# The attention denominators as four array tiles of 32 columns, with one reciprocal and a spread by DMA

## Chip, cores, metric

One core of one Trainium2 chip. The metric is the device time of one execution in microseconds, the median of several executions.

## The reference, cut to what matters

A batch of 32 graphs with 512 nodes and 512 features passes two layers. The change lies in the first, an attention with 8 heads of 64 features under an adjacency mask, in 32-bit floats throughout:

```python
scores = einsum('bqhd,bkhd->bhqk', q, k) / sqrt(64)
scores = scores + (1.0 - adj)[None, None, :, :] * -1e9
attn = softmax(scores, axis=-1)
out = einsum('bhqk,bkhd->bqhd', attn, v).reshape(b, n, d)
x = x + (out @ Wo + bo)
```

## The kernel before

The softmax has no maximum subtracted; it is exp of masked scores, and the division comes after the product with the values. Two heads, a *pair* of heads j of 4, are handled together: head s of the pair has partitions 64s to 64s+63. For each pair and batch (128 times) there are

- `scores`: keys on partitions, 512 queries along the row; the mask added by VectorE, exp by ScalarE, and the four exps of a pair summed by VectorE into `es`;
- `values`: the product with v into the bank `po`, copied by ScalarE to `o`;
- `finish`: the denominators. The sum of `es` over its 128 partitions is a product with a matrix of ones, which also copies the sum to 64 rows of each head, just where `o` has that head's features. PSUM (`psum.tile`) is the memory that takes TensorE's results, used here in banks of 512 columns.

```python
def finish(b, j, st):
    need("rd")
    pd = psum.tile([P, N], F32, name=f"pd_{b}_{j}", tag="pd")
    for s in range(2):
        nc.tensor.matmul(
            pd[s * HD : (s + 1) * HD, :], ones[:, :HD], st["es"][j][:, s, :], start=True, stop=True
        )
    pe(0.95)
    o = st["o"][j // 2][:, j % 2, :]
    rd = wtile([P, N], f"rd_{b}_{j}", "rd", 1)

    def divide(k):
        nc.vector.reciprocal(rd[:, ts(k, H)], pd[:, ts(k, H)])
        if k:
            then("rd", rest)

    def rest():
        junk = wtile([P, N], f"rj_{b}_{j}", "rj", 1, BF16)
        nc.scalar.activation(junk, rd, AF.Copy, accum_out=rsum[:, b, j : j + 1])
        nc.gpsimd.tensor_tensor(o, o, rd, op=ALU.mult)

    finished.add((b, j))
    release()
    for k in range(2):
        later("rd", 0.0, gap(b, (j + 1) % NP) + 3.0, 1.7, lambda k=k: divide(k))
```

Here P is 128, N is 512, H is 256 and HD is 64. The order of each engine's instructions is set by hand, with a small model of time while the program is built: `pe(us)` says that TensorE has so much more work, `later(key, wait, by, cost, fn)` lets a VectorE instruction go in where the model finds room, and `then(key, fn, wait)` puts out what follows VectorE's work. None of these numbers is a wait on the chip; they set order alone. What an engine waits for on the chip are semaphores, in the order of its own instructions.

The queries of the next batch are multiplied by an edge mask before scores can use them:

```python
nc.gpsimd.tensor_tensor(qh, qh, edge8[:, ts(k, H)], op=ALU.mult)       # proj_q
```

and in the output projection (`out_proj`) GpSimd adds one partial product to the residual, after which VectorE adds further ones from PSUM and so frees the bank that TensorE's last product of that projection needs:

```python
nc.gpsimd.tensor_tensor(r, r, q, op=ALU.add)                           # more(q_)
nc.vector.scalar_tensor_tensor(r, p_, 1.0 / VS, r, op0=ALU.mult, op1=ALU.add)   # add(i, k, p)
```

Another GpSimd instruction is the second layer's last addition, `y += x1`, ahead of the store of the output.

Of the kernel before, what the change touches and what calls it, by code (L numbers as in the profile page):

```python
# [9 lines left out]
F32 = mybir.dt.float32  # L10
BF16 = mybir.dt.bfloat16
I32 = mybir.dt.int32
AF = mybir.ActivationFunctionType
# [7 lines left out]
P = 128  # L21
HD = 64
# [13 lines left out]
H = 256  # L36
# [25 lines left out]
def kernel(  # L62
# [23 lines left out]
    nc = tc.nc  # L86
    B, N, D = x.shape
    T = N // P
    C = D // P
    NP = D // P  # L90
# [3 lines left out]
    def ctile(shape, name, dt=F32):  # L94
        return const.tile(shape, dt, name=name, tag=name)
# [8 lines left out]
    ones = ctile([P, P], "ones")  # L104
# [18 lines left out]
    rsum = ctile([P, B, NP], "rsum")  # L123
# [24 lines left out]
    psum = fast.enter_context(tc.tile_pool(name="psum", bufs=1, space=bass.MemoryType.PSUM))  # L148

    def wtile(shape, name, tag, bufs, dt=F32):  # L150
        return work.tile(shape, dt, name=name, tag=tag, bufs=bufs)
# [7 lines left out]
    def run_spare(i):  # L159
        _, ready, cost, fn, _ = spare.pop(i)  # L160
        clock["dve"] = max(clock["dve"], ready) + cost
        fn()

    def pe(us):

        clock["pe"] += us
        till = clock["pe"] + (1.0 if at_ends[0] else 0.4)
        while True:
            due = [i for i, (_, t, _) in enumerate(ends) if t <= till]
            fits = [  # L170
                (by, i) for i, (_, t, cost, _, by) in enumerate(spare)
                if max(clock["dve"], t) + cost <= till
            ]
            if due:
                ends.pop(due[0])[2]()
            elif fits:
                run_spare(min(fits)[1])
            else:
                return
# [5 lines left out]
    def later(key, wait, by, cost, fn):  # L185

        now = max(clock["dve"], clock["pe"])
        spare.append((key, now + wait, cost, fn, now + by))

    def then(key, fn, wait=0.0):  # L190

        ends.append((key, clock["dve"] + wait, fn))

    def need(key):

        waits = at_ends[0] and key not in ("e", "es") and any(e[0] == key for e in spare + ends)
        run_all(key)
        if waits:
            clock["pe"] = max(clock["pe"], clock["dve"])
# [326 lines left out]
    def release():  # L526
        while held:
            held.pop(0)()

    def gap(b, j):  # L530
        return GAPS.get(b, GAP)[j]
# [68 lines left out]
    def finish(b, j, st):  # L600

        need("rd")
        pd = psum.tile([P, N], F32, name=f"pd_{b}_{j}", tag="pd")
        for s in range(2):
            nc.tensor.matmul(  # L605
                pd[s * HD : (s + 1) * HD, :], ones[:, :HD], st["es"][j][:, s, :], start=True, stop=True
            )
        pe(0.95)
        o = st["o"][j // 2][:, j % 2, :]
        rd = wtile([P, N], f"rd_{b}_{j}", "rd", 1)  # L610

        def divide(k):
            nc.vector.reciprocal(rd[:, ts(k, H)], pd[:, ts(k, H)])  # L613
            if k:
                then("rd", rest)

        def rest():
            junk = wtile([P, N], f"rj_{b}_{j}", "rj", 1, BF16)
            nc.scalar.activation(junk, rd, AF.Copy, accum_out=rsum[:, b, j : j + 1])  # L619
            nc.gpsimd.tensor_tensor(o, o, rd, op=ALU.mult)  # L620

        finished.add((b, j))
        release()
        for k in range(2):
            later("rd", 0.0, gap(b, (j + 1) % NP) + 3.0, 1.7, lambda k=k: divide(k))

    def residual(b, st, i, tag="x1", bufs=3):

# [198 lines left out]
    def denominators(b, j):  # L827
        done = (b, j - 1) if j else (b - 1, NP - 1)
        if done[0] in states:
            finish(*done, states[done[0]])  # L830
# [336 lines left out]
```

## Time and profile before

| | before |
|---|---|
| median | 3678.0 us (3676.8 to 3679.0) |
| one batch in the steady part | 112.12 us, of which TensorE is busy 111.67 |
| denominators' product, start to next start | 0.910 us |
| GpSimd's multiply after the second reciprocal | 0.14 us in three places of a batch, 3.40 in one |

The steady part is about 28 of 32 batches; there a batch's period repeats to 0.01 us. The prediction below shows the lines and how they are read.

### The profile page before, as it was taken

How to read it: one execution, taken by the hardware profiler on the slowest of the kernel's cores; microseconds unless marked ns; L12 is line 12 of the kernel's file. 1: busy time of each engine (PE TensorE's matmuls, PEld its weight loads, DVE VectorE, ACT ScalarE, POOL GpSimd, SP SyncE). 2: the span in 40 equal slices, each digit the busy share in tenths (PEclk: the TensorE clock that was granted, in tenths of full speed). 3: DMA queues.
4: the chain of work that ended last, by engine and by line, in shares of the span. 5: the costliest groups of instructions: out<-in, count | busy, mean ns of one | idle time of the engine just before them, and what ended most of it. 6: DMA issues, size and time to landing. Idle time of an engine off the chain costs nothing. (4 is left out here: it accounts for less than half of the span.)

```text
span 3676.4 us, 58866 instructions
## 1 busy us (share of the span) xinstructions
PE 3606.2 (98%) x24310; PEld 1875.1 (51%) x24310; DVE 2802.5 (76%) x4119; ACT 1398.2 (38%) x2086; POOL 1147.1 (31%) x965
## 2 busy tenths in 40 slices
PE   9999999999999999999999999999999999999986
PEld 5545554555554555545555545555455555455532
DVE  6977777787777877777877778777778777787783
ACT  3433334334333433343333334333434343343331
POOL 5423333223333222332233332323332333323241
PEclk9999999999999999999999999999999999999998
DMA  3001111101111011111011110011110111100100
GB/s 130 18 7 35 38 38 35 33 9 38 38 38 35 10 32 38 38 35 38 4 38 38 38 35 14 28 38 38 35 38 4 38 38 38 35 18 24 32 27 27
DMA packets 71074, 120.58 MB, mean 33 GB/s; under 512 B 11856, under 2 KB 15952, under 8 KB 70800
## 3 DMA queue, kind: packets, MB, share of 16 engines
q1 hardware_dynamic: 69216, 114.91, 9.9%
q8 instruction: 193, 3.16, 0.4%
q10 hardware_dynamic: 1376, 1.57, 0.1%
q14 instruction: 81, 0.66, 0.1%
q0 software_dynamic: 208, 0.27, 0.0%
HBM read 83.11 MB, written 33.62 MB: 32 GB/s over the span
## 5 line engine op out<-in xcount | busy, mean ns | idle before, releaser
L620 POOL TENSOR_TENSOR oT<-oT,rd 128x512 f32<-128x512 f32 x128 | 167.2, 1306 | 1527.1 <-DVE rd L613 1524.5
L567 ACT ACTIVATE e<-e 128x1024 f32<-128x1024 f32 x512 | 541.0, 1057 | 196.0 <-DVE e L552 160.0
L552 DVE TENSOR_TENSOR e<-ps,nmT 128x1024 f32<-128x1024 f32 x384 | 455.1, 1213 | 101.9 <-PE ps L542 101.8
L542 PE MATMUL ps<-qT,kT 64*128 64x512 f32 x2048 | 483.4, 606 | 12.7 <-DVE e L552 12.7
L590 PE MATMUL po<-e,v 128*64 128x512 f32 x2048 | 463.1, 593 | 0.0
L51 PE MATMUL pg<-at,hn 128*64 128x512 f32 x2048 | 449.7, 598 | 13.2 <-DVE dmax L775 13.2
L51 PE MATMUL py<-w,gT 128*64 128x512 f32 x2048 | 447.4, 595 | 0.1
L613 DVE RECIPROCAL rd<-pd 128x256 f32<-128x256 f32 x256 | 435.0, 1729 | 0.0
L804 POOL TENSOR_TENSOR y<-y,x 128x512 f32<-128x512 f32 x128 | 193.2, 1509 | 544.9 <-DVE y L802 489.9
L542 PEld LDWEIGHTS ps<-qT,kT 64*128 64x128 f32 x2048 | 184.2, 186 | 309.4 <-issue 214.9
L564 DVE TENSOR_TENSOR es<-es,e 128x1024 f32<-128x1024 f32 x254 | 316.6, 1246 | 13.2 <-ACT e L567 0.6
L51 PEld LDWEIGHTS pg<-at,hn 128*64 128x64 f32 x2048 | 148.9, 138 | 307.5 <-issue 307.5
L51 PEld LDWEIGHTS py<-w,gT 128*64 128x64 f32 x2048 | 148.1, 138 | 293.9 <-issue 292.3
L590 PEld LDWEIGHTS po<-e,v 128*64 128x64 f32 x2048 | 157.8, 138 | 235.1 <-issue 225.4
L598 ACT COPY oT<-po 128x512 f32<-128x512 f32 x128 | 73.8, 576 | 388.2 <-PE po L590 388.2
L714 DVE CUSTOM_DVE_ANT_0 scr<-hn,wa_r 128x512 f32<-128x512 f32 x256 | 169.9, 719 | 49.0 <-ACT hn L701 49.0
L619 ACT ACTIVATE rj<-rd 128x512 bf16<-128x512 f32 x128 | 80.7, 630 | 327.5 <-DVE rd L613 327.4
L741 ACT ACTIVATE at<-at 128x512 f32<-128x512 f32 x128 | 80.4, 628 | 286.3 <-DVE at L737 286.3
L800 ACT ACTIVATE y<-py,rd 128x512 f32<-128x512 f32 x128 | 87.6, 685 | 261.2 <-PE py L51 253.0
L564 DVE TENSOR_TENSOR es<-e,e 128x1024 f32<-128x1024 f32 x127 | 180.9, 1424 | 0.7 <-PE pd L605 0.7
L639 POOL TENSOR_TENSOR x<-x,c_row 128x512 f32<-128x512 f32 x128 | 176.9, 1403 | 0.0
L321 POOL TENSOR_TENSOR rs<-rs,mhalf 128x2 f32<-128x2 f32 (+1 forms) x97 | 78.7, 811 | 306.9 <-DVE rs L320 305.8
(189 smaller groups left out, 5726.5 us busy)
## 6 DMA issues: line engine op xcount, KB each, us to landing
x<-in_x_dram SPq DMA_DIRECT2D x128, 256.0 KB, 3.0
out_dram<-y SPq DMA_DIRECT2D x128, 256.0 KB, 2.1
x<-in_x_dram SPq DMA_DIRECT2D x63, 512.0 KB, 4.2
s<-row_s SPq DMA_DIRECT2D x32, 256.0 KB, 4.2
adj<-in_adj_dram SPq DMA_DIRECT2D x4, 256.0 KB, 7.1
w<-in_L_gnn_W_dram SPq DMA_DIRECT2D x1, 1024.0 KB, 7.9
wk<-in_L_gnn_Wk_dram ACTq DMA_DIRECT2D x3, 256.0 KB, 8.9
wq<-in_L_gnn_Wq_dram SPq DMA_DIRECT2D x3, 256.0 KB, 7.6
```

The lines of the kernel that those rows point to most:

```text
L51: nc.tensor.matmul(out[s : s + HD], lhsT[:, s : s + HD], rhs, start=start, stop=stop, skip_group_check=onto)
L542: nc.tensor.matmul(ps[s], st["kT"][j][rows, ts(k, P)], st["qT"][j][rows, :], start=True, stop=True)
L552: nc.vector.tensor_tensor(e, p, nmT[:, k, :].unsqueeze(1).to_broadcast([P, 2, N]), op=ALU.add)
L564: (nc.gpsimd if early else nc.vector).tensor_tensor(es, one, e, op=ALU.add)
L567: nc.scalar.activation(e, e, AF.Exp)
L590: nc.tensor.matmul(po[s * HD : (s + 1) * HD, :], v[k // 2][:, k % 2, (2 * j + s) * HD : (2 * j + s + 1) * HD], e[k][:, s, :], start=k == 0 ...
L613: nc.vector.reciprocal(rd[:, ts(k, H)], pd[:, ts(k, H)])
L620: nc.gpsimd.tensor_tensor(o, o, rd, op=ALU.mult)
L639: nc.gpsimd.tensor_tensor(r[:, t, :], r[:, t, :], c_row, op=ALU.add)
L714: nc.vector.tensor_tensor_reduce(scr, st["hn"][t], r, 1.0, 0.0, op0=ALU.mult, op1=ALU.add, accum_out=st["s12"][:, g, t : t + 1],)
L800: nc.scalar.activation(y, p, AF.Exp, scale=r)
L804: nc.gpsimd.tensor_tensor(y, y, x1_of(st, t), op=ALU.add)
```

## The change

Its intent: with 32 columns of ones in place of 64, four tiles of the array can work at once, each on one head and one half of the queries. TensorE then streams 256 columns in place of 512. The result is [128, 256], so one reciprocal does for two. But each quarter of 32 rows now holds one head's and one half's denominators and has to be brought to two groups of 32 rows each of `rd`: eight DMAs.

```diff
-        pd = psum.tile([P, N], F32, name=f"pd_{b}_{j}", tag="pd")
+        pd = psum.tile([P, N], F32, name=f"pd_{b}_{j}", tag="pd")[:, :H]
         for s in range(2):
-            nc.tensor.matmul(
-                pd[s * HD : (s + 1) * HD, :], ones[:, :HD], st["es"][j][:, s, :], start=True, stop=True
-            )
-        pe(0.95)
+            for k in range(2):
+                r = (2 * s + k) * 32
+                nc.tensor.matmul(
+                    pd[r : r + 32, :], ones[:, :32], st["es"][j][:, s, ts(k, H)], start=True, stop=True
+                )
+        pe(0.5)
         o = st["o"][j // 2][:, j % 2, :]
-        rd = wtile([P, N], f"rd_{b}_{j}", "rd", 1)
-        def divide(k):
-            nc.vector.reciprocal(rd[:, ts(k, H)], pd[:, ts(k, H)])
-            if k:
-                then("rd", rest)
+        rq = wtile([P, H], f"rq_{b}_{j}", "rq", 1)
+        def divide():
+            nc.vector.reciprocal(rq, pd)
+            then("rd", rest)
         def rest():
-            junk = wtile([P, N], f"rj_{b}_{j}", "rj", 1, BF16)
-            nc.scalar.activation(junk, rd, AF.Copy, accum_out=rsum[:, b, j : j + 1])
+            nc.scalar.activation(pd, rq, AF.Copy, accum_out=rsum[:, b, j : j + 1])
+            rd = wtile([P, N], f"rd_{b}_{j}", "rd", 1)
+            for s in range(2):
+                for k in range(2):
+                    r = (2 * s + k) * 32
+                    for h in (s * HD, s * HD + 32):
+                        nc.sync.dma_start(rd[h : h + 32, ts(k, H)], rq[r : r + 32, :])
             nc.gpsimd.tensor_tensor(o, o, rd, op=ALU.mult)
-        for k in range(2):
-            later("rd", 0.0, gap(b, (j + 1) % NP) + 3.0, 1.7, lambda k=k: divide(k))
+        later("rd", 0.0, gap(b, (j + 1) % NP) + 3.0, 1.7, divide)
```

## The prediction

> **What bounds the kernel now.** I read the page's busy shares first, then the two last full periods before the middle of the run (one batch each, cut at the start of the same denominators' product in successive batches), then the list of TensorE's own waits, then the timeline around one denominators' product.
>
> ```profile
> PE 3606.2 (98%) x24310; PEld 1875.1 (51%) x24310; DVE 2802.5 (76%) x4119; ACT 1398.2 (38%) x2086; POOL 1147.1 (31%) x965
> ```
> ```profile
> 1309.70:1421.82 112.13, 111.68 (x754) 58.16 (x753) 86.51 (x128) 43.56 (x66) 34.23 (x29) 1.00 0.10 31
> 1421.82:1533.94 112.12, 111.67 (x754) 58.20 (x753) 86.52 (x128) 43.56 (x66) 34.22 (x29) 1.00 0.10 31
> ```
> ```profile
> PE pg L51 <- DVE dmax L775: 13.2, 2, 11.1
> PE ps L542 <- DVE e L552: 12.7, 32, 1.5
> PE pe L51 <- DVE as L748: 10.6, 1, 10.6
> PE pd L605 <- DVE rd L613: 10.4, 2, 5.5
> ```
>
> In the windows the first figure after the stretch is its length, the next TensorE's busy time, then weight loads, VectorE, ScalarE and GpSimd. A batch takes 112.12 us and TensorE works 111.67 of them; VectorE 86.52, so it has some 25 us free per batch. The period repeats to 0.01 us, so no variable wait lies in it. TensorE's waits for other engines sum to under 60 us in the whole run, and the two on the reciprocal (line 613, 10.4 us) are single events in batch 1 and in the tail. So the steady stage is bound by TensorE's stream; only what shortens the stream shortens the time, and 32 x 112.12 = 3588 of 3678 us are that stage.
>
> The product that is changed, with what stands before and after it:
>
> ```profile
> 1530.31 3.71 PE L542 MATMUL ps<-qT,kT 64*128 64x512 f32 x16
> 1533.94 1.08 PE L605 MATMUL pd<-es,ones 128*64 128x512 f32 x4
> 1534.86 1.90 PE L51 MATMUL x_k<-hT,wk 128*64 128x256 f32 x16
> ```
> ```profile
> 1533.94 0.20 PEld L605 LDWEIGHTS pd<-es,ones 128*64 128x64 f32 x4 [0.76 <-issue]
> ```
>
> Modelled ends overlap, so I count from start to start: 1534.86 - 1533.94 = 0.91 us is what the product takes from the stream (median of all 128: 0.910). It is 2 matmuls, but 4 records: each 32-bit matmul runs as two passes. The single records start at 0, 7, 481 and 488 ns: both column tiles' first passes together, then both second passes. A following slot of the same shape takes 429 ns for 512 columns and 215 ns for 256. The first slot is 52 ns longer, and the two weight loads of one tile start 54 ns apart, so this is the first load of 64 columns, which nothing hides. The last score slot before it is 519 ns and not 429: about 92 ns when the layout of the array changes (64 rows by 128 columns to 128 by 64). Wherever the layout changes in this trace I find that same 92 to 94 ns (scores to product, product to scores, to and from the transposes), followed by a longer first slot; where the products have one shape there is neither.
>
> **What the Trainium skill says.** (1) "TensorEngine Tiling (Array Packing)", Key Properties: a change of tiling mode drains the engine, and different tiles load weights and multiply in parallel. The trace agrees: the 92 ns above, and two tiles that start 7 ns apart. That page lists 128x32 with four tiles. (2) "TensorE: Matmul & The Clock Gate", LDWEIGHTS: a load takes its columns over 1.2 per ns, 53 ns for 64; the trace has 54. For 32 columns that is 27 ns, an estimate. (3) The same page, Measured speedup vs the span model: three column tiles of 32 gained 2.38x. No part of the kernel before uses four tiles, so this case doesn't yet show that four run abreast. (4) "DMA: Bandwidth & Descriptors", Anatomy of one DMA: a fixed cost of about 2 us for each. The trace has 2.1 us from issue to landing for 256 KB out, 1.4 for 2 KB.
>
> **The change part by part.**
>
> TensorE. Four tiles of 32 columns with 256 queries each in place of two of 64 with 512. If all four run abreast: first slot 215 + 27 = 242 ns, second 215, four starts 7 ns apart 14 ns more than two; 471 ns. But products before and after are in 128x64, and now the array changes twice: the drain ahead of it is already paid after scores, a new one of 93 ns follows, and the next product's first slot becomes 52 ns longer. 471 + 93 + 52 = 616 ns in place of 910: 0.294 us saved for each, 128 x 0.294 = 37.6 us. In four cases the product follows a 128x64 product and the front change is new too: 4 x 0.145 = 0.6. Net 37.0 us, all on the path that sets the end.
>
> VectorE.
>
> ```profile
> L613 DVE RECIPROCAL rd<-pd 128x256 f32<-128x256 f32 x256 | 435.0, 1729 | 0.0
> L620 POOL TENSOR_TENSOR oT<-oT,rd 128x512 f32<-128x512 f32 x128 | 167.2, 1306 | 1527.1 <-DVE rd L613 1524.5
> L619 ACT ACTIVATE rj<-rd 128x512 bf16<-128x512 f32 x128 | 80.7, 630 | 327.5 <-DVE rd L613 327.4
> ```
>
> One reciprocal of 128x256 in place of two: 128 x 1.73 = 221 us less VectorE, 6.9 us a batch. It lies beside TensorE, which waits for VectorE 0.4 us a batch at most, so it is worth nearly nothing in the steady stage. In batch 1 and the tail, where the product waited 5.5 and 4.9 us for the earlier reciprocal, some 1.7 us each can come back. ScalarE's check runs over 256 elements in place of 512: by its 630 ns some 0.2 us less each, off the path.
>
> DMA. Eight issues a product from SyncE, 1024 in all, 32 KB each, 32 MB together on a queue that has 10% of the engines' time.
>
> ```profile
> 1512.81 0.33 SPq L805 DMA_DIRECT2D out_dram<-y  x1
> 1516.79 0.86 SPq L328 DMA_DIRECT2D x<-in_x_dram  x2
> ```
> ```profile
> out_dram<-y SPq DMA_DIRECT2D x128, 256.0 KB, 2.1
> row_s<-s SPq DMA_DIRECT2D x32, 2.0 KB, 1.4
> ```
>
> Issues back to back come some 0.4 us apart: 8 x 0.4 = 3.2 us, and about 1.8 us for the last to land. GpSimd's multiply can start 5.0 us after the reciprocal in place of 0.14; the one reciprocal less takes 1.7 back, so 3.3 us later. What follows on GpSimd waits with it. Per batch the four places are: the combinations for the output projection, finished 35 us before their use; the residual's bias, not urgent; the combinations for the keys, of which the first is wanted about 10 us after it is ready; and the queries' multiply by the edge mask, ready at 1447.7 where the scores start at about 1450.8, 3 us of slack with some gap between the two multiplies to absorb part of the delay. So the delay mostly hides; I put 5 us in all (0.15 us a batch) for places where it doesn't. In the tail the combinations after the last product do set TensorE's start (a wait of 3.7 us at line 51), so about 3 us are lost there against some 5 us that the reciprocals free in head and tail: net 2 us gained.
>
> Sum: 3678.0 - 37.0 - 2.0 + 5.0 = 3644.0 us.
>
> **The rivals.**
>
> First, the four tiles don't run abreast. The passes stand in the program tile by tile, and a queue that looks past only one blocked pass would give pairs: three slots (242 + 215 + 215 = 672, + 145 = 817 ns), 0.09 us saved, 12 us: about 3669 with the rest. Two full pairs one after the other: 242 + 3 x 215 + 145 = 1032 ns, 16 us slower: about 3697. For it: nothing here shows four tiles. Against it: after each change of layout four weight loads start within 61 ns and the second tile's first pass overtakes the first tile's second. A milder form: the diagonal's products of 64 columns take 119 ns a slot of two records, some 60 ns each, not their streaming time. If that is a floor for each record, a slot of four is 238 ns: 0.25 saved, 3650.
>
> Second, the transfer becomes the bound. SyncE's queue is in order, and the rd pieces can stand behind a store that waits for GpSimd, or the row of logits (line 134), for which the queue waited 745 us in 32 times. Then GpSimd stands still, with it the queries or the variance's power, and VectorE behind that, and the scores. 1 us a batch would be 32 us, about 3676; beyond that it turns slower. For it: small slack at the queries. Against it: the multiply already waited 1524.5 us for the reciprocal in 110 cases without reaching TensorE, and VectorE has 7 us more room a batch.
>
> Third, VectorE's relief shows. If the 221 us had been holding TensorE, time could fall by over 100 us. The 0.45 us per batch in which TensorE is not busy speaks against it.
>
> **Range and chances.** Four abreast, delays hidden: 3630 to 3650, some 65%. The record floor or a partial overlap: 3650 to 3672, 15%. Four not abreast, or the transfer in the way: 3670 and up, 17%. Better than 3628 needs more than the stream can give. So 3628 to 3684 for 8 in 10. Over 2% faster is under 3604.5: 0.57 us from each product of 0.91, more than its four-tile form leaves; 0.03. Over 2% slower is above 3751.6: 2.3 us lost in each batch, only with the transfer in the way; 0.05.
>
> **What would show it.** Right: starts of the eight matmul records within some 25 ns in two groups 240 ns apart, 0.62 us from the product's start to the next one's, a 52 ns longer first slot in what follows; a period of about 110.9 us at a TensorE share still above 99%; VectorE near 80 us a batch; eight transfers 0.4 us apart and the multiply some 5 us after the reciprocal, with no new wait on TensorE's list. Wrong: three or four groups of starts; a wait of the scores on queries or mask sums that comes from GpSimd; a period that varies from batch to batch.

## The result, and the profile after

3853.8 us (3840.0 to 3860.2, four runs) against 3678.0: ratio 1.0473, 95% interval 1.0443 to 1.0503, slower by 4.7%. (Ratios are the mean time of one kernel's runs over that of the other's of the same rounds, so not quite the ratio of the medians.) The result is correct.

First the product itself, in the timeline of TensorE and of its weight loads of the changed kernel (start us, length us, engine, line, operation, operands):

```profile
1141.61 0.64 PE L608 MATMUL pd<-es,ones 128*32 128x256 f32 x8
1142.18 1.95 PE L51 MATMUL x_k<-hT,wk 128*64 128x256 f32 x16
```
```profile
1141.61 0.16 PEld L608 LDWEIGHTS pd<-es,ones 128*32 128x32 f32 x8 [0.76 <-issue]
```

From start to next start 0.57 us (median of all 128: 0.569), where 0.91 was. The eight records start at 0, 7, 13, 20 and 240, 247, 253, 260 ns: four tiles abreast. The first slot after it is 52 ns longer. This is what was predicted, to 5 ns. Yet the whole is slower. The busy shares, and two periods of one batch:

```profile
PE 3615.3 (94%) x24822; PEld 1783.0 (46%) x24822; DVE 2601.7 (68%) x3991; ACT 1370.8 (36%) x2086; POOL 1257.8 (33%) x965
```
```profile
1022.56:1141.61 119.05, 113.63 (x771) 55.82 (x769) 79.72 (x124) 42.50 (x66) 37.06 (x29) 0.97 0.12 38
1141.61:1258.00 116.39, 110.46 (x754) 54.45 (x752) 78.17 (x120) 40.98 (x63) 36.67 (x27) 0.97 0.13 39
```

The period is longer and no longer constant (115 to 120 us), TensorE stands idle 5.4 and 5.9 us of it, and its granted clock (the third number from the end) is 0.97 in place of 1.00. TensorE's list of waits (us in all, times, longest), whose first two rows are new:

```profile
PE qz_w L51 <- DVE x L666: 83.0, 29, 3.8
PE ps L542 <- POOL qT L485: 63.2, 29, 3.1
PE ps L542 <- DVE e L552: 21.3, 24, 3.1
```

29 times each, once a batch: the last product of the output projection waits 2.9 us for VectorE to free its bank, and the scores wait 2.2 us for GpSimd's edge multiply of the queries. The second is quickest to follow. GpSimd's timeline before, then the changed kernel's, at the same place of a batch:

```profile
1441.59 1.27 POOL L620 TENSOR_TENSOR oT<-oT,rd 128x512 f32<-128x512 f32 x1 [21.18 <-DVE rd L613]
1444.63 1.41 POOL L485 TENSOR_TENSOR qT<-qT,edge 128x256 f32<-128x256 f32 x2 [1.77 <-DVE qT L481]
1446.29 1.42 POOL L485 TENSOR_TENSOR qT<-qT,edge 128x256 f32<-128x256 f32 x2 [0.24 <-DVE qT L481]
```
```profile
1048.93 1.50 POOL L627 TENSOR_TENSOR oT<-oT,rd 128x512 f32<-128x512 f32 x1 [28.18 <-DMA rd<-rq]
1050.40 4.12 POOL L485 TENSOR_TENSOR qT<-qT,edge 128x256 f32<-128x256 f32 x4
```

Before, GpSimd had done the multiply by 1442.9 and took the queries as VectorE delivered them. Now it stands until 1048.93 in front of a multiply whose `rd` is still in flight, while the queries pile up behind it, and does all four in one stretch to 1054.5. SyncE and TensorE at that moment:

```profile
1039.62 1.75 DVE L616 RECIPROCAL rq<-pd 128x256 f32<-128x256 f32 x1
1041.40 5.86 SPq L626 DMA_DIRECT2D rd<-rq  x8
1053.88 2.93 PE L542 MATMUL ps<-qT,kT 64*128 64x512 f32 x6 [2.73 <-POOL qT L485]
```

One DMA holds SyncE for 0.59 us in the median (0.34 for a store of the output), so eight issues stand 4.35 us from first start to last start; the multiply starts another 2.26 us later. Over the steady part the median from the reciprocal's end to the multiply is 6.7, 8.0, 6.9 and 6.7 us in the four places of a batch.

The other wait has the same root. At the second place GpSimd stood 6.94 us for the transfers (1122.78), and the residual's addition (line 682), on which VectorE's additions and with them the bank depend, came after it. GpSimd before, then GpSimd, VectorE and TensorE in the changed kernel, each in one batch:

```profile
1519.97 1.27 POOL L620 TENSOR_TENSOR oT<-oT,rd 128x512 f32<-128x512 f32 x1
1521.20 2.50 POOL L676 TENSOR_TENSOR x<-x,q_w 128x512 f32<-128x512 f32 x2
```
```profile
1122.78 1.27 POOL L627 TENSOR_TENSOR oT<-oT,rd 128x512 f32<-128x512 f32 x1 [6.94 <-DMA rd<-rq]
1124.01 1.27 POOL L810 TENSOR_TENSOR y<-y,x 128x512 f32<-128x512 f32 x1
1125.24 2.51 POOL L645 TENSOR_TENSOR x<-x,c_row 128x512 f32<-128x512 f32 x2
1127.70 1.27 POOL L386 TENSOR_TENSOR uT<-uT,oT 128x512 f32<-128x512 f32 x1
1128.92 2.50 POOL L682 TENSOR_TENSOR x<-x,q_w 128x512 f32<-128x512 f32 x2
1130.22 0.69 DVE L666 SCALAR_TENSOR_TENSOR x<-qz_w,x 128x512 f32<-128x512 f32 x1 [4.58 <-POOL x L682]
1130.97 2.83 PE L51 MATMUL qz_w<-wo,uT 128*64 128x256 f32 x16 [2.69 <-DVE x L666]
```

In both kernels the order differs between batches: the addition follows the multiply at once, or after four other instructions, as here. It is late either way. Counted from the second `x_w<-wo,oT` of the same projection on TensorE (1519.87 and 1122.93 here), it starts 1.3 us later before (25 batches, 1.0 to 1.3) and 6.2 us later in the changed kernel (24 batches, 5.6 to 7.0).

A third loss follows the waits. After some of them the trace's clock records grant TensorE half its rate for 3.41 us at a time. One such stretch in the windows view:

```profile
1131.90:1135.30 3.40, 3.40 (x15) 1.45 (x13) 2.54 (x6) 0.00 (x0) 3.24 (x3) 0.50 0.00 0
```

It follows a wait for the bank that ended at 1130.97; TensorE counts as busy in all of it, at a clock of 0.50. Between 300 and 3500 us there are 71.7 us of such stretches, each after a wait at one of the two places; before there are none. At half rate they cost up to 35.8 us of progress (some begin as much as 0.5 us before the wait ends), and this doesn't stand in any list of waits.

Per batch, from starts in the trace (a group's time runs to the start of the next group, so a wait counts to the group ahead of it; mean of 26 batches, us; e1 and e2 are experiments below):

| group | before | changed | e1 | e2 |
|---|---|---|---|---|
| denominators' product | 3.64 | 2.29 | 2.28 | 2.28 |
| scores | 15.14 | 15.64 | 14.54 | 14.54 |
| values (the wait for qT follows) | 14.19 | 16.61 | 14.16 | 14.16 |
| projection, y bank (the wait for the bank follows) | 1.73 | 4.80 | 1.73 | 1.73 |
| projection, its two products `qz_w<-wo,uT` (the last one waited) | 3.45 | 4.04 | 3.45 | 3.45 |
| whole period | 112.12 | 117.48 | 110.22 | 110.22 |

### The profile page after: what moved, and what is told of

The parts are those of the page before. It is cut to its first block, busy times and chain, and to the rows that moved or that the text cites. A ratio compares the mean times of both kernels' runs of the same rounds, so it can differ in the third digit from the quotient of the medians. Undisturbed runs are those within 1.5% of the kernel's fastest.

```text
span 3838.2 us, 61981 instructions
## 1 busy us (share of the span) xinstructions
PE 3615.3 (94%) x24822; PEld 1783.0 (46%) x24822; DVE 2601.7 (68%) x3991; ACT 1370.8 (36%) x2086; POOL 1257.8 (33%) x965
## 5 line engine op out<-in xcount | busy, mean ns | idle before, releaser
L627 POOL TENSOR_TENSOR oT<-oT,rd 128x512 f32<-128x512 f32 x128 | 184.8, 1444 | 2041.2 <-DMA rd<-rq 1988.8
L542 PE MATMUL ps<-qT,kT 64*128 64x512 f32 x2048 | 493.8, 618 | 84.4 <-POOL qT L485 63.2
L810 POOL TENSOR_TENSOR y<-y,x 128x512 f32<-128x512 f32 x128 | 235.7, 1842 | 389.8 <-DVE y L808 357.8
L564 DVE TENSOR_TENSOR es<-es,e 128x1024 f32<-128x1024 f32 x254 | 338.9, 1334 | 12.8 <-DVE es L564 0.5
L616 DVE RECIPROCAL rq<-pd 128x256 f32<-128x256 f32 x128 | 224.3, 1752 | 18.1 <-issue 10.4
L51 PE MATMUL qz_w<-wo,uT 128*64 128x256 f32 x1040 | 140.9, 419 | 83.0 <-DVE x L666 83.0
L346 DVE TENSOR_SCALAR x<-x,mv,rs 128x512 f32<-128x512 f32 x128 | 82.1, 687 | 138.3 <-POOL rs L321 138.2
L793 ACT COPY gT<-pg 128x512 f32<-128x512 f32 x128 | 75.0, 586 | 257.6 <-PE pg L51 257.6
L645 POOL TENSOR_TENSOR x<-x,c_row 128x512 f32<-128x512 f32 x128 | 166.2, 1322 | 0.0
```

What stands on the lines that cost most here:

```text
L51: nc.tensor.matmul(out[s : s + HD], lhsT[:, s : s + HD], rhs, start=start, stop=stop, skip_group_check=onto)
L542: nc.tensor.matmul(ps[s], st["kT"][j][rows, ts(k, P)], st["qT"][j][rows, :], start=True, stop=True)
L564: (nc.gpsimd if early else nc.vector).tensor_tensor(es, one, e, op=ALU.add)
L616: nc.vector.reciprocal(rq, pd)
L645: nc.gpsimd.tensor_tensor(r[:, t, :], r[:, t, :], c_row, op=ALU.add)
L810: nc.gpsimd.tensor_tensor(y, y, x1_of(st, t), op=ALU.add)
```

## The experiments

Theory T: the loss is the time from reciprocal to multiply, in which GpSimd, which works in order, holds up what TensorE needs. Rivals: the new code order (O); the denser array or the two changes of its layout (C); the transfers themselves, by SyncE's queue or their traffic (S).

### e1: no transfer

```diff
-            rd = wtile(...)  and the eight dma_start
-            nc.gpsimd.tensor_tensor(o, o, rd, op=ALU.mult)
+            nc.gpsimd.tensor_tensor(
+                o.rearrange("p (k h) -> p k h", k=2), o.rearrange("p (k h) -> p k h", k=2),
+                rq.unsqueeze(1).to_broadcast([P, 2, H]), op=ALU.mult)
```

> The changed kernel without the eight transfers: GpSimd multiplies by the reciprocal where it lies, both halves of the queries by the same 256 values (a wrong result on purpose; the same product, reciprocal, check and code order). Theory T, that the loss is the transfer, which holds the in-order GpSimd 6.7 to 8 us after each reciprocal: the gain of the product remains, 3678 - 37 = about 3640 us, and the waits of the scores on qT (63 us) and of qz_w (83 us) are gone. Rival O, that the new code order (other costs in the order model) makes the waits: stays above 3780. Rival C, that the denser array or the two changes of layout lower the clock or cost more than counted: stays above 3700.

3613.6 us (3612.4 to 3616.0), ratio to before 0.9827, wrong result. Both waits are gone. The order of instructions is that of the changed kernel and the product is the new one, so O and C are out as the main cause: with them alone the kernel is 63 us faster than before. The transfer path costs 3853.8 - 3613.6 = 240 us. That 63 is well over the 37 expected is taken up at e8.

### e2: the multiply later in GpSimd's queue

```diff
-            nc.gpsimd.tensor_tensor(o, o, rd, op=ALU.mult)
+            then("rd", lambda: nc.gpsimd.tensor_tensor(o, o, rd, op=ALU.mult), 7.0)
```

> The changed kernel with GpSimd's multiply put into its queue 7 us (of the order model) after the transfers are issued, so that other GpSimd work goes first; same transfers, correct result. Theory T: the wait is taken off GpSimd's path, most of the loss goes, 3640 to 3680 us. Rival S, that the transfers harm by themselves (SyncE's queue delays the loads and stores, or their writes slow the engines' reads): stays above 3780. Rival O: unclear, as this also changes the order.

3632.2 us (3631.0 to 3634.1), ratio 0.9879, correct, 8 us below the range expected. The multiply still starts 6.7 to 8.5 us after the reciprocal in the median of each place, the same transfers are issued 0.62 us apart, and the period is that of e1:

```profile
1000.00:1110.22 110.22, 110.22 (x772) 54.66 (x770) 78.87 (x124) 42.52 (x66) 36.12 (x29) 1.00 0.13 42
```

So S is out: it is not the traffic and not the queue, but what stands behind the multiply on GpSimd. One line makes the change a gain. The 18.6 us between e2 and e1 lie in head and tail, where there is nothing to put ahead of the multiply: up to the eleventh product e2 takes 304.5 us and e1 300.3, and from the 119th to the end 350.3 and 338.1.

### e3 and e5: the kernel before with the transfers alone

```diff
-            nc.scalar.activation(junk, rd, ...)
-            nc.gpsimd.tensor_tensor(o, o, rd, op=ALU.mult)
+            nc.scalar.activation(pd, rd, ...)
+            rq = wtile([P, H], f"rq_{b}_{j}", "rq", 1)
+            for h in range(0, P, 32):
+                for k in range(2):       # e3; e5 reads columns H + k * P on, of the second half
+                    nc.sync.dma_start(rq[h : h + 32, ts(k, P)], rd[h : h + 32, ts(k, P)])
+            (multiply by rq for both halves, as in e1)
```

> The kernel before with its own product and its two reciprocals, but with eight transfers of 32 partitions between the reciprocals and GpSimd's multiply (which then reads 256 values twice: a wrong result on purpose), and the check written to the sums' bank as in the changed kernel. Theory T: the loss comes with the transfers alone, at least as large as in the changed kernel, whose stream is 37 us shorter: 3678 + 150 to 220 = 3830 to 3900 us. Rivals O and C: unchanged, 3670 to 3690.

3756.9 us (3756.6 to 3762.1), ratio 1.0223: half the loss expected. The trace says why: these transfers read only what the first of the two reciprocals writes, start 1.5 us before the second ends, and the multiply came 5.0 us after it (in three of the four places; some 6.3 in the second).

> As e3_before_with_transfer (the kernel before, its own product, eight transfers ahead of GpSimd's multiply, a wrong result on purpose), but the transfers read the half that the second reciprocal writes, so that the first of them can't start before it has ended. In e3 they started 1.5 us ahead of it, and the multiply 5.0 us after it in place of 6.7 in the changed kernel; the loss was 80 us. Theory T: the loss grows with those 1.7 us, towards the 240 us that the changed kernel loses against e1: 3840 to 3900 us. Rival: a loss that depends on the number of transfers and not on when they land: stays at 3757.

3933.5 us (3929.0 to 3941.8), ratio 1.0698, 256 us over before and above the range expected. The multiply came 6.6 us after the reciprocal (8.1 in the second place), and the two waits of the changed kernel are there, in the old array layout and with two reciprocals:

```profile
PE qz_w L51 <- DVE x L666: 89.4, 29, 4.3
PE ps L542 <- POOL qT L485: 65.6, 29, 3.2
```

So the transfers make them alone. And 1.6 us more of delay (5.0 to 6.6) took the loss from 80 to 256 us. The two waits grew from 48 us in e3 (39.2 for the bank, 9.0 for qT) to 155, and the half-rate stretches between 300 and 3500 us from 3.4 to 122.9 us, worth up to 60. So the loss is no fixed price of the transfers: slack is used up first, and beyond it the clock adds to the waits.

### e4: the changed kernel in the order of before

```diff
-        pe(0.5)
+        pe(0.95)
...
-        later("rd", 0.0, gap(b, (j + 1) % NP) + 3.0, 1.7, divide)
+        for k in range(2):           # divide(0) does nothing, divide(1) the one reciprocal
+            later("rd", 0.0, gap(b, (j + 1) % NP) + 3.0, 1.7, lambda k=k: divide(k))
```

> The changed kernel with the order model's costs of the kernel before (0.95 us for the product, two places for the reciprocal), so GpSimd's instructions stand in exactly the order of before; same operations. Theory T: within 40 us of the changed kernel, 3815 to 3895 us, with the waits on qT again. Rival O: back near 3640 to 3680 us.

3811.1 us (3802.6 to 3812.0), ratio 1.0358: 4 us below the range, 43 us under the changed kernel. GpSimd's order is that of before (all 965 instructions) and the loss remains, so the order is a small part. The wait on qT was expected and is down to 11.6 us in 12 cases, while that for the bank is 92.3 in 29. The traces show why the first shrank: counted from the first product of the queries (medians of 24 batches), the reciprocal ends 4.7 us after it here and 5.9 in the changed kernel. And the wait follows the moment of the multiply whatever the layout: the multiply starts 6.5 us after that product before, 10.0 in e6 (below), 11.3 in e3, 11.4 in e4, 12.7 in the changed kernel and 13.0 in e5, and the wait on qT is 0, 0, 9.0, 11.6, 63.2 and 65.6 us.

### e6: four transfers in place of eight

```diff
-                    r = (2 * s + k) * 32
-                    for h in (s * HD, s * HD + 32):
-                        nc.sync.dma_start(rd[h : h + 32, ts(k, H)], rq[r : r + 32, :])
+                    h = slice(s * HD, (s + 1) * HD)
+                    nc.sync.dma_start(rd[h, ts(k, H)], rq[h, :])
```

> The changed kernel with four transfers of 64 partitions in place of eight of 32 (the same bytes and the same place of the multiply; a wrong result on purpose, since rows of both quarters are mixed). Theory T with the issue spacing of 0.62 us: the multiply starts 6.7 - 4 x 0.62 = 4.2 us after the reciprocal. The waits of the scores on qT (2.2 us) and of qz_w (2.9 us) appeared at 6.7 to 8 us, so at 4.2 us they should be nearly gone: 3615 to 3670 us. Rival: the bytes or the landing time alone set the loss: within 40 us of 3854.

3649.4 us (3647.4 to 3654.3), ratio 0.9929. The multiply starts 4.1 us after the reciprocal in three places and 5.3 in the second; the wait on qT is gone, that for the bank is 18.4 us in 21 cases. The same bytes in half the issues lose 36 us to e1 in place of 240.

### e7: the multiply later at one place only

```diff
-            nc.gpsimd.tensor_tensor(o, o, rd, op=ALU.mult)
+            if j == 2: then("rd", multiply, 7.0)     # the others at once
```

> The changed kernel with the later multiply (7 us of the order model) only for the product ahead of the queries' edge multiplies; the other three as in the change. Correct result. Theory T: the scores' wait on qT (63 us in all) goes with the half-rate clock after it, qz_w's wait on the residual (83 us) stays: 3740 to 3800 us. If both places hang on one cause elsewhere (SyncE's queue), neither or both go.

3772.5 us (3771.1 to 3775.7), ratio 1.0258, 81 us faster than the changed kernel:

```profile
PE qz_w L51 <- DVE x L670: 82.5, 29, 3.8
PE ps L542 <- DVE e L552: 22.1, 25, 3.1
```

The wait on qT (63.2 us) has gone and the other (83.0) has stayed: two places, each with its own blocked instruction, not one cause elsewhere. The profiled executions, whose waits these are, differ by 64 us (3840.0 and 3775.7; the changed kernel's is the fastest of its four), which is the wait that went. The half-rate stretches are unchanged, 71.7 us between 300 and 3500 us: they now follow the other wait.

### e8, e9, e11: is VectorE's relief worth anything?

e1 and e2 have a period of 110.22 us. The product explains 4 x 0.29 = 1.16 of the 1.90 us gained; scores gained 0.60.

```diff
 e8 (on e2):  later(...) twice, as before; nc.vector.reciprocal(rq, pd) in both places
 e9 (on e8):  the reciprocal in the second place only, all else in the order of e8
 e11 (on e2): for _ in range(2): nc.vector.reciprocal(rq, pd)
```

> e2 with the reciprocal done twice (the second overwrites the first with the same values; correct result), in the two places of before. Theory V: the period of e2 is 110.22 us and not the 110.96 that the product alone explains, because scores waited 0.6 us a batch for VectorE's masks (they took 15.14 us in the kernel before and 14.54 in e2) and one reciprocal less frees those: e8 brings the 0.6 us back, 3632 + 20 = about 3652 us. Rival: the scores gain by the new order or by the earlier product: stays at 3632.

3741.5 us (3740.8 to 3743.1), ratio 1.0176: 109 us over e2, five times the amount expected. It differs from e2 in two things, so both were taken apart:

> e8 without its second reciprocal, every instruction that is left in the same order (correct result). e8 lost 109 us against e2, far more than the 20 expected, and differs from e2 in two things: the second reciprocal and the code order. If VectorE's time is the cause (theory V): back near e2, 3630 to 3650 us. If the order is: stays above 3700 us.

> e2 with a second reciprocal right after the first, order and order model as in e2 (correct result). Theory V as first sized: scores wait some 0.6 us a batch more for VectorE's masks, 3632 + 20 = 3652 us; if VectorE's time is worth as much as e8 suggests, 3700 to 3745 us; if it isn't on the path at all, 3632.

e9: 3672.6 us (3672.4 to 3674.9), ratio 0.9990. e11: 3710.8 us (3709.5 to 3712.7), ratio 1.0091. So the second reciprocal costs 69 us in the order of e8 (3741.5 - 3672.6) and 79 us in that of e2 (3710.8 - 3632.2), and the order of e8 costs 40 us on its own (3672.6 - 3632.2): e9 met neither of its two expectations. In e11 scores take 15.63 us a batch against 14.54 in e2. That is less than half of its longer period (112.60 against 110.22): 1.06 us more lie between the second and the third product of the output projection, where TensorE waits for GpSimd's addition of the residual's bias (26.7 us in 22 cases; none in e2). Nor is e11 VectorE's time alone, for its second reciprocal also holds back the transfers by 1.75 us; in e8 and e9 the reciprocal that starts them stands in the same place. The 69 us in turn hold half-rate stretches of 34.1 us in e8 (3.4 in e9), worth up to 15. The lists of waits for the masks, on the weight loads, of before, e2 and e11:

```profile
PEld ps L542 <- DVE e L552: 82.1, 128, 2.4
```
```profile
PEld ps L542 <- DVE e L552: 64.4, 128, 3.9
```
```profile
PEld ps L542 <- DVE e L552: 101.4, 128, 3.9
```

Of these totals 64.4 us stay in e2, where the matmuls of the scores wait only 6.0 us for the masks, so the total is not the loss; the 17.7 us between before and e2 match the 0.60 us a batch that scores gained. An engine that is busy 71% of the time can be on the path: the masks are due at fixed moments, and a reciprocal of 1.75 us in front of one of them delays scores. How much of the changed kernel's own 0.60 us comes from less work and how much from its order stays open.

### e10: the best version found

e2, with batches 0, 1 and 31 done as before (product of two tiles, two reciprocals, no transfer), since the delay can't hide there.

```diff
+        if b < 2 or b == B - 1:
+            return finish_ends(b, j, st)      # finish() of before, its check written to pd
```

> e2, but batches 0, 1 and the last take the denominators' product, the two reciprocals and the multiply as in the kernel before, since there the 6.7 us of transfer can't hide: e2 was 4 us behind e1 before the first steady batch and 12 us in the tail (correct result). Expected 3632 - 4 to 12 = 3620 to 3628 us; if the ends don't depend on the transfer, 3632.

3623.4 us (3621.8 to 3624.7), ratio 0.9853 (0.9837 to 0.9869), correct: 1.5% faster than the kernel before and 6.0% than the changed one (3623.4 / 3853.8 = 0.940).

## Why the prediction was wrong, point by point

- *TensorE, 37.0 us.* Right, in mechanism and size. Four tiles start within 20 ns, the slot is 0.569 us where 0.564 was counted, and what follows is 52 ns longer. The first rival, tiles that don't run abreast, is refuted. Its milder form, a floor for each record, is not: the first slot's 240 ns are 215 and 25 for the first load of 32 columns, but also four times 60, and two slots of 238 and the 145 for the changes of layout are 621 ns, as measured (the 0.25 us saved that it names don't follow from its slot). For the load speaks that the first slots of the products with 64 columns and of the scores with 128 are 52 and 105 ns longer too.
- *The transfer, multiply 3.3 us later, so that the delay mostly hides.* This is the step that failed. Issues were counted 0.4 us apart from those of loads and stores; from SBUF to SBUF they are 0.62 (4.35 us for seven intervals), and landing and GpSimd's four pairs of semaphores 2.26 and not 1.8: 6.7 us and not 5.0. And most of the 1.7 us credited for the missing reciprocal was not there at the place that mattered: VectorE does the one reciprocal later than the first of the two. Measured from the same product of the queries on TensorE (start 1440.31 before, 1040.64 after), the reciprocal ends 1.1 us and 0.7 us after it: a gain of 0.4. The multiply starts 1.3 us after it before and 8.3 after: 7.0 us later where 3.3 was counted. e6 comes near the delay that was counted: its multiply is 3.5 us later there than before (10.0 against 6.5), and it took 3649.4 us, close to the 3644.0 predicted. In part that is luck: 18.4 us of waits for the bank stand against a gain at the scores (0.57 us a batch) that the prediction didn't have.
- *Slack at the queries.* 3 us with "some gap" was about right: the scores waited 2.7 us of those 7.0, so some 4.3 us were hidden, and e6 at 4.1 us shows no such wait.
- *The residual's bias, not urgent.* Wrong by omission. At the same place stands the residual's partial sum, on which VectorE and a PSUM bank depend; that wait is the larger of the two (83.0 us). I had followed GpSimd's consumers, but not the consumers of these; and I had taken 0.14 us from reciprocal to multiply for all places, where this one had 3.40.
- *5 us for what doesn't hide.* The path cost 240 us (changed kernel against e1), 224 in the profiled executions (3840.0 and 3616.0). In these the two waits hold 146 us and the half-rate clock behind them up to 36. Of the other 42, the scores' waits for VectorE's masks are 17 (21.3 us against 4.4 in e1); the rest I did not divide. The clock had no place in the prediction.
- *The second rival* named this way to the slower side: the multiply not landed, GpSimd still, with it the queries, and then scores. It put 1 us a batch on it as the likely size and 0.05 on slower by 2%. Its argument against, that the multiply already waited 1524.5 us for the reciprocal without reaching TensorE, doesn't hold: before, GpSimd stood there with nothing due behind it, since the multiply had ended 1.77 us before the first of the queries came (1442.86 and 1444.63). A long wait of an engine says nothing about how much longer it may last. Its other form, rd's issues behind a store or the row of logits, didn't occur: the first issue started 0.07 us after the reciprocal in three of four places and 1.2 in the fourth.
- *VectorE, worth nearly nothing.* Wrong, in the favourable direction. A second reciprocal costs 69 to 79 us in two other orders; what its absence is worth in the changed kernel's own order no run shows. I read TensorE's waits from the matmul rows alone, where the masks have 12.7 us; on the weight loads the same wait has 82.1, of which 17.7 went. The third rival, over 100 us, did not come true (e1 gained 63, 37 of them the product's), but its mechanism was nearer than I allowed.

## What to carry to other kernels

Before a transfer goes between a producer and an in-order engine, write down what stands behind the consumer in that engine's queue, when each of it is due, and who waits for it in turn; the slack of the next deadline, here some 4 us, is what the whole path (issues, landing, semaphores) may cost. "DMA: Bandwidth & Descriptors", Rules for kernel authors, of the Trainium skill says it as issuing the DMA early and waiting for its semaphore late: moving one instruction back by 7 us in the queue turned 3853.8 us into 3632.2 with the same work. And an engine at 70 to 76% busy need not be free: try a doubled instruction before calling its time worthless.

## What the Trainium skill lacked or had wrong

- "TensorE: Matmul & The Clock Gate", Part 1, has the clock halve after at least one idle window of some 3.4 us. Here stretches of 3.41 us at half rate began after, or up to 0.5 us before the end of, gaps of 2.46 to 4.13 us from one matmul's start to the next's, the streaming of the first included (20 of 58 such gaps over 1.8 us between 300 and 3400 us): waits of 2 us are enough at times.
- No page has the issue time of a transfer from SBUF to SBUF on SyncE ("DMA: Bandwidth & Descriptors", where it belongs, tells copies on this chip apart neither by direction nor by size there): 0.59 us for 32 or 64 partitions of 1 KB, against 0.34 for a store of 128 partitions of 2 KB to DRAM.
- "TensorEngine Tiling (Array Packing)", Key Properties, has that a change of mode drains the engine, but no size: 92 to 94 ns here.
